# Self-attention on one core: a group's last gathers and the rotation of its keys, each one head later

## The chip, the cores and the metric

The kernel runs on one core of a Trainium2 chip. The time is device time in microseconds of one execution, and the median of several executions is compared. The core's engines work side by side, each through its own instructions in order: TensorE (PE, with weight loads PEld), VectorE (DVE), ScalarE (ACT), GpSimd (POOL) and SyncE (SP, which here only issues DMAs). They wait for each other through semaphores.

## The reference

One decoder layer in float32 on 32 sequences of 64 tokens with 512 features, taken as 2048 tokens: self-attention, cross-attention and a feed-forward part, each with a residual and a layer norm behind it. The change lies in self-attention:

```
NH, NKV, HD = 32, 8, 128;  BLOCK, NBLK, TOPK = 32, 128, 16
q, k, v = x @ wq.T, x @ wk.T, x @ wv.T          # 32, 8 and 8 heads of 128
q, k = apply_rope(q), apply_rope(k)             # one rotation for all tokens
k_full = concat(k_cache[block_idx], k[0])       # 16 cached blocks of 32 keys,
v_full = concat(v_cache[block_idx], v[0])       # and the 64 tokens of sequence 0
attn = softmax(q @ k_full.T / sqrt(HD))         # 576 keys for each query
out = (attn @ v_full) @ wo.T
```

Four query heads share one key and value head. The cached keys and values are the same for all tokens, so they are fetched once for each of the 8 groups.

## The kernel before, in words

Self-attention takes 128 steps, the loop `for n in range(N)`. A step is one head of one block of 512 tokens: 8 groups `g`, in each 4 blocks of tokens `tb`, in each 4 heads `h`. In the text a step's place within its group is `r = n % 16`, called head 0 to head 15.

A head has four tiles of 128 queries. `scores(n, i)` multiplies one tile with the 576 keys into a PSUM tile `s` of two banks (L615), of which the pool `sc` has two; DVE takes the negated maximum (`nmax`, L620); ACT takes the exponential into `p` (L623) and sums it; DVE inverts the sum (`den`, L632), scales `p` by it (L633), and transposes `p` in 32x32 blocks into `T` (L641). `move` issues DMAs that lay `T` out as `pT`, and two heads later `values` multiplies `pT` with the values into `po` (L661). Between the four tiles stand steps of two projections, at L282: the queries of the next block (`q_...`, one step `q`) and the output projection of the last block (`w_...`, step `w`). Both are Strassen-like products of seven multiplications, whose sums of operands are made on POOL: `token_sums` gives `tx` (L196 to L199) at the end of each block, `output_sums` gives `so` (L256 to L259), and the sums of a new group's output weights `wo` come at heads 5 and 6. DVE reads the products back into `qT` and `acc` (L299 to L325, L345, L353).

While group `g` is computed, the keys and values of group `g + 1` are made ready:

- `load_group` at head 4 loads the two weight slices on ACT's queue.
- `gather_keys(g + 1, t)` makes row indices on DVE (`row`, L538, one column for each `t`) and issues an indirect DMA on POOL that fetches 128 rows of cached keys into `kn` (L523). `gather_values(g + 1, t)` does the same for the values into `v`. There are four of each, `t` = 0 to 3. The keys' call stands at the start of a head, the values' between its tiles 2 and 3.
- `rotate(g + 1)` turns the 4 x 128 gathered keys: POOL multiplies the odd elements (L557), DVE makes three products (L558 `kq`, L559 `kr`, L560 `kt`), POOL subtracts (L561), DVE adds (L562).
- `new_keys` (twelve small matmuls, L576 and L582, and two copies on ACT) and `cached_keys` (transposes of the rotated keys, L596) are put into the list `later`, from which `spare_bank` takes one in every even head, after the first step.

PE and DVE run in the order in which the code is written (`manual_schedule` with these two engines). The order of POOL, ACT and SP is made by the scheduler of the framework from dependencies and place in the code. On POOL in head 7 of a group with gathers it is: token sums L197 and L198, gather of keys, gather of values, token sum L199, rotation product L557; then in head 8 the output sum L258 and the rotation's L561.

Of the kernel before, what the change touches and what calls it, by code (L numbers as in the profile page):

```python
# [18 lines left out]
NH, NKV, HD = 32, 8, 128  # L19
REP = NH // NKV  # L20
# [32 lines left out]
def decoder_layer(  # L53
# [49 lines left out]
    def token_room(b, name):  # L103
        return act.tile([P, NC, TB], F32, tag=f"xT{b % 2}", name=name)

    def load_features(dst, src, tb, queue=nc.sync):
        queue.dma_start(
            out=dst, in_=src[:, tb * TB : (tb + 1) * TB].rearrange("(c p) n -> p c n", p=P)
        )
# [9 lines left out]
    def bank(shape, name, tag=None):  # L119
        if tag in special:  # L120
            v = special[tag]
            return v.rearrange("p (a b) -> p a b", a=shape[1])
        return psum[-1].tile(shape, F32, tag=tag or "ps", name=name)
# [340 lines left out]
    with ExitStack() as ph:  # L464
# [47 lines left out]
        def load_group(g, queue=nc.scalar):  # L512
            ws = []
            for tag, src in (("wk", wkT), ("wv", wvT)):
                w = kv.tile([P, NC, HD], F32, tag=tag, name=f"{tag}{g}", bufs=1)
                queue.dma_start(
                    out=w, in_=src[:, g * HD : (g + 1) * HD].rearrange("(c p) n -> p c n", p=P)
                )
                ws.append(w)
            wkv_cur[g] = ws  # L520

        def gather(g, dst, src, t):
            nc.gpsimd.indirect_dma_start(  # L523
                out=dst[:, t, :], out_offset=None, in_=src,
                in_offset=bass.IndirectOffsetOnAxis(ap=rows_cur[g][:, t : t + 1], axis=0),
            )

        def gather_keys(g, t):
            if t == 0:
                rows_cur[g] = kv.tile([P, NKT], I32, tag="row", name=f"row{g}")  # L530
                kn_cur[g] = kv.tile([P, NKT, HD], F32, tag="kn", name=f"kn{g}", bufs=1)
                kr_cur[g] = kv.tile([P, NKT, HD], F32, tag="kr", name=f"kr{g}", bufs=1)
                vs[g] = kv.tile([P, NKC, HD], F32, tag="v", name=f"v{g}")
            if g == 0:
                if t == 0:
                    nc.vector.tensor_scalar(rows_cur[g], row_f, 0.0, None, ALU.add)
            else:
                nc.vector.tensor_scalar(  # L538
                    rows_cur[g][:, t : t + 1], row_f[:, t : t + 1], float(g), None, ALU.add
                )  # L540
            gather(g, kn_cur[g], k_rows, t)

        def gather_values(g, t):
            gather(g, vs[g], v_rows, t)

        def rotate(g, t0=0, t1=NKT):


            kn = kn_cur[g][:, t0:t1, :].rearrange("p t (d two) -> p t d two", two=2)
            k4 = kr_cur[g][:, t0:t1, :].rearrange("p t (d two) -> p t d two", two=2)  # L550
            shape = [P, t1 - t0, HD // 2]
            c3 = cs[:, None, :].to_broadcast(shape)
            s3 = sn[:, None, :].to_broadcast(shape)
            tmp = kv.tile(shape, F32, tag="tmp", name=f"kt{g}_{t0}", bufs=1)
            tmq = kv.tile(shape, F32, tag="tmq", name=f"kq{g}_{t0}", bufs=1)
            e, o = kn[:, :, :, 0], kn[:, :, :, 1]
            nc.gpsimd.tensor_tensor(k4[:, :, :, 1], o, c3, ALU.mult)  # L557
            nc.vector.tensor_tensor(tmq, e, s3, ALU.mult)  # L558
            nc.vector.tensor_tensor(k4[:, :, :, 0], e, c3, ALU.mult)  # L559
            nc.vector.tensor_tensor(tmp, o, s3, ALU.mult)  # L560
            nc.gpsimd.tensor_tensor(k4[:, :, :, 1], k4[:, :, :, 1], tmq, ALU.subtract)  # L561
            nc.vector.tensor_tensor(k4[:, :, :, 0], k4[:, :, :, 0], tmp, ALU.add)  # L562
# [29 lines left out]
        def cached_keys(g, tag="po1"):  # L592
            kr = kr_cur.pop(g)
            pt = bank([P, NKT, P], f"pkt{g}", tag)
            for t in range(NKT):
                nc.tensor.transpose(pt[:, t, :], kr[:, t, :], ident)  # L596
            dst = kTs[g].rearrange("p (s b k) -> p s b k", s=2, k=SQ)
            for r0, b0 in ((0, 0), (2, SHARED + 1)):
                nc.scalar.activation(
                    dst[:, :, b0 : b0 + NKT, :],  # L600
                    pt[:, :, r0 * SQ : (r0 + 2) * SQ].rearrange("p t (s k) -> p s t k", s=2),
                    AF.Copy, scale=SCALE,
                )
# [96 lines left out]
        def columns(g):  # L700
            return slice(g * REP * HD, (g + 1) * REP * HD)
# [39 lines left out]
        def flush():  # L741
            while reads:
                reads.pop(0)()
# [55 lines left out]
        def last_products(i):  # L799
            if i == 3:  # L800
                first.mul("z", 3)
                reads.append(lambda: nc.vector.tensor_tensor(c[0, 1], z, c[0, 1], ALU.add))
            elif i == 7:
                first.mul("y", 7)
                reads.append(lambda: nc.vector.tensor_tensor(c[1, 1], y, c[1, 1], ALU.add))
            else:
                first.mul("y", 4)
                reads.append(lambda: nc.vector.tensor_tensor(c[1, 0], y, c[1, 0], ALU.add))
# [6 lines left out]

        for n in range(N):
            b, h = divmod(n, REP)
            g, r = units[n][0], n % PER  # L820
            if r == REP and g + 1 < NKV:
                load_group(g + 1)
            if r // REP == 1 and g + 1 < NKV:
                gather_keys(g + 1, h)
            if r == 2 * REP and g + 1 < NKV:
                rotate(g + 1)
                later.append(lambda g=g: new_keys(g + 1))
            if r == 2 * REP + 1 and g + 1 < NKV:
                later.append(lambda g=g: cached_keys(g + 1))
            if n == N - REP:  # L830
                encT[0] = big.tile([P, NC, TB], F32, tag="qT", name="encT0", bufs=2)
                load_features(encT[0], encT_in, 0)
            steps = {0: "qwqw", 1: "qw q", 2: "wqwq", 3: "w qw"}[h]

            def step(place):
                if n < REP:

                    i = {(0, 0): 3, (0, 1): 7, (0, 3): 4}.get((n, place))
                    if i:
                        last_products(i)  # L840
                    elif (n, place) in ((0, 2), (1, 0), (1, 1), (1, 2), (1, 3), (2, 0), (2, 2)):
                        q_step(n)
                elif steps[place] == "q":
                    q_step(n)
                elif steps[place] == "w":
                    w_step(b - 2 if h < 2 else b - 1)
                flush()

            def spare_bank():

                if n % 2 == 0 and later:
                    later.pop(0)()

            scores(n, 0)
            step(0)
            spare_bank()
            scores(n, 1)
            if 0 < n < REP:

                move(n - 1, (3,), nc.scalar)  # L860
            if n >= 2:
                values(n - 2, 0, 2 if n % 2 == 0 else 3)
            step(1)
            scores(n, 2)
            step(2)
            if r // REP == 1 and g + 1 < NKV:
                gather_values(g + 1, h)
            scores(n, 3)
            if n >= 2:
                values(n - 2, 2 if n % 2 == 0 else 3, NKT)  # L870
                if n % 2:
                    shared_values(n - 2)
            step(3)
            spare_bank()
            if h == REP - 1:
                if b + 2 < NB:
                    g2, tb2, _ = units[(b + 2) * REP]
                    if tb2 == 0:
                        wq_cur[g2] = load_left(wqT[:, columns(g2)], f"wq{g2}", nc.gpsimd)
                    tok[b + 2] = token_sums(xTs.pop(b + 2), f"tx{g2}_{tb2}", nc.gpsimd)  # L880
                elif b + 2 == NB:
                    kvw[0] = load_kv_left(0, "wq")
                else:
                    encR[0] = token_sums(encT[0], "te0", nc.gpsimd)
            if h == REP - 1 and b + 3 < NB or n == 0:

                b2 = b + 3 if n else 2
                xTs[b2] = token_room(b2, f"xT{b2}")
                load_features(xTs[b2], xT_in, b2 % NTB)
            move(n, (0, 1, 2) if n < REP - 1 else range(NQD))  # L890
# [47 lines left out]
    with ExitStack() as ph:  # L938
# [283 lines left out]
        for n in range(N + 1):  # L1222
            if n < N:
                g, tb = units[n]
# [106 lines left out]
```

## Time and profile before

| | us |
|---|---|
| median of 3 runs | 3100.44 (3098.5 to 3103.58) |
| the profiled execution | 3099.28 |
| its span, first to last instruction | 3097.0 |
| PE busy | 3038.2 (98%) |
| DVE busy | 2184.0 (71%) |
| POOL busy | 967.6 (31%) |
| the scaling of p at L633, 512 times, median and longest of one | 0.520, 2.970 |
| a gather of keys on POOL, 32 times, median; from issue to landing | 0.958; 5.9 to 7.2 |

The page gives for each engine the time in which it was busy, and for groups of instructions the mean of one and the idle time of the engine before them. A line of the timeline has the start, the duration, the engine, the line of the kernel, the operation, what it writes and reads, shapes and count, and in brackets the idle time before it with the instruction that ended it. A line of the view of waits has who waited for whom, the total in us, how often, and the longest. Spans on POOL are rough.

### The profile page before, as it was taken

To read this page: it belongs to the slowest core of one execution; us is meant where nothing else is said; L and a number is where in the kernel's file an instruction comes from. 1 tells how busy PE (TensorE), PEld (TensorE's weight loads), DVE (VectorE), ACT (ScalarE), POOL (GpSimd) and SP (SyncE) were. 2 spreads that over 40 slices of the span, in tenths; PEclk is the share of its full clock that TensorE was granted. 3 is DMA by queue.
4 is the path that set the end of the run, shared out by engine and by line. 5 is a ranking of instruction groups with operands and counts; after the bars stand their busy time and mean duration, and the time that the engine had idled before them with its cause. 6 is when DMAs were issued, how large, how long until landed. Compare 5 with 4: busy or idle time off the path is not lost.

```text
span 3097.0 us, 42303 instructions
## 1 busy us (share of the span) xinstructions
PE 3038.2 (98%) x14944; PEld 2318.1 (75%) x14944; DVE 2184.0 (71%) x3957; ACT 754.8 (24%) x1760; POOL 967.6 (31%) x789
## 2 busy tenths in 40 slices
PE   8999999999999999999999999999999999999998
PEld 6777677777777777777677769988888888888864
DVE  6777777877877877877877754346656656656777
ACT  2323222222222232232322321211111111111132
POOL 4231321321322322323222122135444444444421
PEclk9999999999999999999999999999999999999999
DMA  6444444444444444444344343321121121121101
GB/s 206 116 114 119 113 115 123 111 122 114 108 128 112 106 128 113 107 125 118 101 123 109 98 126 128 109 103 48 50 67 48 51 66 48 51 66 48 49 28 41
DMA packets 200913, 298.66 MB, mean 96 GB/s; under 512 B 44160, under 2 KB 94848, under 8 KB 200704
## 3 DMA queue, kind: packets, MB, share of 16 engines
q1 hardware_dynamic: 187328, 282.51, 33.7%
q10 hardware_dynamic: 11328, 9.26, 1.0%
q0 software_dynamic: 2048, 4.20, 0.5%
q8 instruction: 120, 1.97, 0.3%
q14 instruction: 89, 0.73, 0.1%
HBM read 107.05 MB, written 20.97 MB: 41 GB/s over the span
## 4 chain that ended last, share of the span: by engine, by line
PE 86%; DVE 10%; DMA 1%; SPq 1%; issue 1%; ACT 1%; DVEq 0%; ACTq 0%
PE po L661 15%; PE s L615 15%; PE pox L1103 2%; DVE acc L345 2%; SPq L653 1%; PE w_0y L282 1%; PE q_3y L282 1%; PE w_3y L282 1%; PE qx_3y L282 1%; PE qx_2y L282 1%; PE qx_0y L282 1%; PE q_2y L282 1%; PE w_1y L282 1%; PE qx_1y L282 1%; PE wx_3y L282 1%; PE q_0y L282 1%
## 5 line engine op out<-in xcount | busy, mean ns | idle before, releaser
L623 ACT ACTIVATE p<-s,nmax 128x576 f32<-128x576 f32 x512 | 379.2, 741 | 1211.6 <-DVE nmax L620 1173.1
L615 PE MATMUL s<-kT,qT 128*128 128x288 f32 x2048 | 578.0, 408 | 11.5 <-ACT p L623 10.7
L661 PE MATMUL po<-pT,v 128*128 128x512 f32 (+1 forms) x1280 | 549.1, 602 | 4.3 <-DMA pT<-T 4.3
L615 PEld LDWEIGHTS s<-kT,qT 128*128 128x128 f32 x2048 | 387.4, 190 | 116.4 <-issue 20.1
L620 DVE TENSOR_REDUCE nmax<-s 128x1 f32<-128x576 f32 x512 | 384.0, 750 | 47.5 <-PE s L615 45.3
L641 DVE STREAM_TRANSPOSE T<-p 128x576 f32<-128x576 f32 x512 | 394.0, 769 | 4.4
L661 PEld LDWEIGHTS po<-pT,v 128*128 128x128 f32 (+1 forms) x1280 | 213.7, 189 | 204.2 <-issue 176.9
L633 DVE TENSOR_SCALAR p<-p,den 128x576 f32<-128x576 f32 x512 | 325.5, 636 | 17.9
L632 DVE RECIPROCAL den<-den 128x1 f32<-128x1 f32 x512 | 83.9, 164 | 238.2 <-ACT p L623 220.0
L256 POOL TENSOR_TENSOR so<-oT,oT 128x512 f32<-128x512 f32 x32 | 42.6, 1330 | 651.0 <-ACT oT L684 651.0
L258 POOL TENSOR_TENSOR so<-oT 128x512 f32<-128x512 f32 x32 | 40.7, 1272 | 334.4 <-PE w_1y L282 93.0
L1209 POOL TENSOR_TENSOR txx<-x1T 128x512 f32<-128x512 f32 x31 | 39.3, 1267 | 244.4 <-PE qx_3z L282 94.1
L197 POOL TENSOR_TENSOR tx<-xT 128x512 f32<-128x512 f32 x31 | 39.7, 1280 | 206.9 <-PE q_3z L282 65.5
L623 ACT ACTIVATION_READ_ACCUMULATOR p<-s,nmax 128x1 f32 x512 | 99.0, 193 | 0.0
L1059 ACT ACTIVATE ex<-ex 128x512 f32<-128x512 f32 x64 | 39.3, 630 | 203.1 <-DVE ex L1058 203.1
L256 POOL TENSOR_TENSOR sox<-oTx,oTx 128x512 f32<-128x512 f32 x32 | 40.5, 1266 | 149.7 <-DVE oTx L1123 144.3
L684 ACT COPY oT<-po 128x512 f32<-128x512 f32 x128 | 71.8, 586 | 44.9 <-PE po L661 44.1
L1043 PEld LDWEIGHTS sx<-kvx,qTx 128*64 128x64 f32 x2048 | 62.3, 138 | 10.6 <-issue 10.6
L1121 ACT ACTIVATE oTx<-pox,bv 128x256 f32<-128x256 f32 x128 | 52.0, 470 | 66.4 <-PE pox L1103 66.4
L1043 PE MATMUL sx<-kvx,qTx 128*64 128x64 f32 x2048 | 66.7, 224 | 0.0
L1103 PE MATMUL pox<-pTx,kvx 64*128 64x256 f32 x512 | 64.5, 389 | 0.1
L1123 DVE TENSOR_SCALAR oTx<-pox,bv 128x256 f32<-128x256 f32 x128 | 53.6, 478 | 9.8 <-PE pox L1103 9.8
(445 smaller groups left out, 5779.9 us busy)
## 6 DMA issues: line engine op xcount, KB each, us to landing
pT<-T SPq DMA_DIRECT2D x1020, 80.0 KB
pT<-T SPq DMA_DIRECT2D x1016, 64.0 KB
xT<-in_xT SPq DMA_DIRECT2D x31, 1024.0 KB
kvx<-kv SPq DMA_DIRECT2D x32, 512.0 KB
pTx<-Tx SPq DMA_DIRECT2D x256, 64.0 KB
kv<-c SPq DMA_DIRECT2D x30, 512.0 KB
wo<-in_woT SPq DMA_DIRECT2D x32, 256.0 KB
xwq<-in_xwq SPq DMA_DIRECT2D x32, 256.0 KB
```

The source lines that it names most:

```text
L256: nc.gpsimd.tensor_tensor(t[1], a[1, 0], a[1, 1], ALU.add)
L282: nc.tensor.matmul(self.banks[b][:, m, :], self.left[i][:, k, m * P : (m + 1) * P], self.right[i][:, k, :], start=(first and m + k == 0), ...
L615: nc.tensor.matmul(s[:, a, :HALF], qTs[n // REP][:, units[n][2], i * P : (i + 1) * P], kTs[g][:, a * HALF : (a + 1) * HALF], start=True, s ...
L620: nc.vector.tensor_reduce(nmax, s[:, :, :HALF], AX.XY, ALU.max, negate=True)
L623: nc.scalar.activation(p.rearrange("q (a k) -> q a k", a=2), s[:, :, :HALF], AF.Exp, bias=nmax, accum_out=den,)
L632: nc.vector.reciprocal(den, den)
L633: nc.vector.tensor_scalar(p, p, den, None, ALU.mult)
L641: nc.vector.transpose(Ts[n][:, :, i, :], ps_.pop((n, i)).rearrange("q (b k) -> q b k", k=SQ))
L661: nc.tensor.matmul(pos[n].rearrange("d (a q) -> d a q", a=NQD), vs[units[n][0]][rows, v, :], pTs[n // 2][rows, :, chunk, :], skip_group_ch ...
L684: nc.scalar.copy(o[:, i, :].rearrange("d (t a k) -> d a t k", t=TPB, a=NQD), pos.pop(n - 1 + i).rearrange("d (a t k) -> d a t k", a=NQD, t ...
L1043: nc.tensor.matmul(s[b * SEQ : (b + 1) * SEQ, i * REP + h, :], qTs[n][:, h, pr * HF + c0 : pr * HF + c0 + SEQ], kvs[n][:, pr, 0, c0 : c0 + ...
L1103: nc.tensor.matmul(po[pr, b][:, i, :].rearrange("d (h a j) -> d h a j", h=REP, a=2), kvs[n][r, pr, 1, i * HD : (i + 1) * HD], pTs[n][r, :, ...
```

## The change

Four steps of the preparation are placed otherwise, in each of the seven groups that prepare a next one. The gathers of keys and values number 3 go from head 7, the last of the second block of tokens, to head 8, the first of the third block. The rotation goes from the start of head 8 to the start of head 9. Gathers 0 to 2 stay at heads 4 to 6, the new keys at head 8, the transposes of the cached keys at head 10.

```
+        gathers = {4: 0, 5: 1, 6: 2, 8: 3}
         for n in range(N):
             b, h = divmod(n, REP)
             g, r = units[n][0], n % PER
             if r == REP and g + 1 < NKV:
                 load_group(g + 1)
-            if r // REP == 1 and g + 1 < NKV:
-                gather_keys(g + 1, h)
+            if r in gathers and g + 1 < NKV:
+                gather_keys(g + 1, gathers[r])
             if r == 2 * REP and g + 1 < NKV:
-                rotate(g + 1)
                 later.append(lambda g=g: new_keys(g + 1))
             if r == 2 * REP + 1 and g + 1 < NKV:
+                rotate(g + 1)
                 later.append(lambda g=g: cached_keys(g + 1))
...
-            if r // REP == 1 and g + 1 < NKV:
-                gather_values(g + 1, h)
+            if r in gathers and g + 1 < NKV:
+                gather_values(g + 1, gathers[r])
```

As built, no instruction is added or dropped, and the orders of PE and of SP's queue are the same. On DVE the last row index (L538) goes from the start of head 7 to that of head 8, and the rotation's four operations from the start of head 8 to that of head 9. On POOL head 7 has the three token sums alone; the output sum L258 of head 8 is followed by the gather of keys, the gather of values, and the rotation's L557 and L561. On ACT the copy of the first query product (L310) goes behind the exponential of head 8's first tile.

## The prediction

> A measurement of this kernel can tell about 0.2% (6.2 us) from no change; the chances below use that bound. Heads are numbered 0 to 15 inside a group (four blocks of four heads), groups 0 to 7, and s(7,1) is tile 1 of head 7. +x is a time from the start of a head, which is its first score matmul.
>
> **What bounds the kernel now.** First the shares and the chain of waits:
>
> ```profile
> PE 3038.2 (98%) x14944; PEld 2318.1 (75%) x14944; DVE 2184.0 (71%) x3957; ACT 754.8 (24%) x1760; POOL 967.6 (31%) x789
> ...
> PE 86%; DVE 10%; DMA 1%; SPq 1%; issue 1%; ACT 1%; DVEq 0%; ACTq 0%
> ```
>
> TensorE (PE) is busy for 98% of the span, so moving work on other engines gains only where PE stands still; that is 59 us in all (3097.0 - 3038.2). So next, whom PE waits for:
>
> ```profile
> PE s L615 <- ACT p L623: 10.7, 10, 1.2
> ```
>
> Ten waits of a score matmul for an exponential. In the timeline of PE, four are at the start and the end of attention; the other six are 1.2 us each, all in one place: head 7 of groups 1 to 6. From score row to score row, head 7 of group 1 lasts from 335.77 to 350.99, 15.22 us; head 7 of group 7, where nothing is gathered for a next group, lasts from 1702.13 to 1715.88, 13.75 us. Groups 2 to 6 have the same 15.22. So PE loses 15.22 - 13.75 = **1.47 us, six times**. The timeline of group 1 shows why:
>
> ```profile
> 338.47 1.13 PE L615 MATMUL s<-kT,qT 128*128 128x288 f32 x4
> ...
> 338.91 0.13 DVE L538 TENSOR_SCALAR row<-row_f 128x1 int32<-128x1 f32 x1
> ...
> 340.58 0.94 POOL L523 DMA_INDIRECT v<-in_v_cache,row  x1 [0.30 <-issue]
> ...
> 340.87 2.97 DVE L633 TENSOR_SCALAR p<-p,den 128x576 f32<-128x576 f32 x1
> ...
> 341.54 1.27 POOL L199 TENSOR_TENSOR tx<-xT,tx 128x512 f32<-128x512 f32 x1
> ...
> 342.77 0.74 POOL L557 TENSOR_TENSOR kr<-kn,cs 128x256 f32<-128x256 f32 x1
> ...
> 344.35 0.74 DVE L620 TENSOR_REDUCE nmax<-s 128x1 f32<-128x576 f32 x1
> ...
> 345.19 0.74 ACT L623 ACTIVATE p<-s,nmax 128x576 f32<-128x576 f32 x1 [4.55 <-DVE nmax L620]
> ...
> 346.07 0.78 PEld L615 LDWEIGHTS s<-kT,qT 128*128 128x128 f32 x4 [1.60 <-ACT p L623]
> 346.07 1.24 PE L615 MATMUL s<-kT,qT 128*128 128x288 f32 x4 [1.20 <-ACT p L623]
> ```
>
> Read it backwards. s(7,3) needs one of two score banks, which the exponential of (7,1) frees; that waits for its maximum; and the maximum stands on DVE behind the scaling of (7,0), which took 2.97 us where the median of 512 is 0.52. Beside the long one, GpSimd (POOL) ran three instructions without a gap: the gather of values, a token sum, the first product of the rotation.
>
> [...] 2.97 instead of 0.52 us beside POOL arithmetic, and the first rotation product of group 0 (two SBUF inputs) took 1.05 instead of 0.53 beside a POOL sum. It also shows that a gather alone does not do it: in head 4 of group 1 the scaling at 296.67 took 0.52 us beside the gather of values at 296.59. [...] bars of 0.94 to 0.96 us, landings 5.9 to 7.2 us after issue.
>
> **The change, part by part.** No instruction is added or removed. Per group, seven times, it moves one row-index operation (DVE 0.13 us), two gathers (POOL 0.96 + 0.94 us, 128 rows each) and the rotation (DVE four operations, POOL two, 0.74 + 0.79 us). The orders of PE and of SP's queue are the same in the two built programs.
>
> *Head 7.* POOL had: two token sums, gather of keys, gather of values, third token sum, first rotation product. It keeps the three token sums; the gathers and the product go behind the next block's first output sum. The third token sum then follows the second, which ends at 338.73, and is over at about 340.0, before the scaling at 340.87. So the scaling should take 0.52 us and everything after it on DVE comes 2.97 - 0.52 = 2.45 us sooner: the exponential of (7,1), over at 346.02, is over at 343.6. s(7,3) can start at +8.94, which is 344.71 (the place of s(7,3) in group 0, 118.45 - 109.51). The spare is 1.1 us. Even if the scaling met the third token sum, it would be as in group 7:
>
> ```profile
> 1705.08 1.27 POOL L199 TENSOR_TENSOR tx<-xT,tx 128x512 f32<-128x512 f32 x1
> ...
> 1705.49 1.17 DVE L633 TENSOR_SCALAR p<-p,den 128x576 f32<-128x576 f32 x1
> ```
>
> 1.17 us, and head 7 lasted 13.75 there. Gain: 6 x 1.47 = **8.8 us**. Group 0 has no such wait (13.75 already) and gains nothing.
>
> *Head 8.* It lasts 16.28 us in all seven groups without a gap on PE: 14.22 plus 2.06 for the new keys' matmuls. Taking the rotation out of it gains nothing. Into it come the row index and two gathers. The same row index and gathers stand at the same place of head 4 in the kernel before (row at +0.81, gather at +1.73, after the same output sum and just behind a load of tokens), with no wait on PE. Cost 0. The first rotation product now starts when the keys land, about +9, and may delay one scaling by up to 0.74 us; PE's extra 2.06 us covers that. On ACT one copy of queries goes behind an exponential that is no longer late: 0. On POOL the output sum now stands ahead of the gathers and waits for nothing new.
>
> *Head 9.* This is the only place that the trace before does not show: the rotation on DVE in a head without new keys. Its price is read in head 8:
>
> ```profile
> 353.37 0.53 DVE L558 TENSOR_TENSOR kq<-kn,sn 128x256 f32<-128x256 f32 x1
> ...
> 355.15 0.42 DVE L562 TENSOR_TENSOR kr<-kr,kt 128x256 f32<-128x256 f32 x1
> 355.50 0.75 DVE L620 TENSOR_REDUCE nmax<-s 128x1 f32<-128x576 f32 x1
> ```
>
> 355.50 - 353.37 = 2.13 us ahead of the maximum of (9,0), and behind it all of head 9's softmax. It will begin 0.57 after the accumulation (352.80 to 353.37), that is at +0.77, so the maximum moves from +1.17 to +2.90: 1.73 later. Head 9 before:
>
> ```profile
> 367.27 1.13 PE L615 MATMUL s<-kT,qT 128*128 128x288 f32 x4
> ...
> 372.23 0.74 ACT L623 ACTIVATE p<-s,nmax 128x576 f32<-128x576 f32 x1 [2.11 <-DVE nmax L620]
> ...
> 375.44 0.69 DVE L345 TENSOR_TENSOR acc<-w_0z,acc 128x512 f32<-128x512 f32 x1 [1.62 <-PE w_0z L282]
> ```
>
> The exponential of (9,1) is read out at 373.06, +5.79; it moves to +7.52, and s(9,3), which needs its bank, starts at +8.94. The spare is 1.4 us. The 1.62 us for which DVE was idle before 375.44 then swallow the delay, so nothing passes to head 10. The rotated keys are next wanted for head 10's transposes, over 13 us later. The keys land by about +9.2 of head 8 (2.0 + 7.2), and the rotation begins 16.28 + 0.77 = 17.05 after its start: 8 us to spare. I take 0 for head 9. Bounds: not below 0, as PE has no gap there; above, the whole 2.13 us if nothing covers it, 7 x 2.13 = 14.9 us.
>
> **Sum.** The profiled execution took 3099.28 us (span 3097.0 and 2.3 around it). 3099.28 - 8.8 = 3090.5. The median of the runs, 3100.44, lies 1.16 above that execution, so the forecast is 3100.44 - 8.8 = **3091.6 us**.
>
> **Rivals.**
> 1. *The stall shrinks but stays* (0.17, with runs that scatter). DVE enters head 7 about 1.7 us behind its place in group 0 (maximum at +3.19 against +1.45), because scalings in head 6 (1.56) and at its end (1.17) met POOL sums that are not moved. If the scaling of (7,0) meets more than the third token sum, half the stall may be left: 3100.4 - 4.4 = 3096. For it: that lateness. Against it: after the third token sum POOL has nothing until the output sum some 10 us later.
> 2. *The rotation loses its cover* (0.09), the one that ends slower. In head 8 the 2.06 us of new-key matmuls hid it; head 9 has none. It decides once the exponential of (9,1) ends after +8.94, which takes 1.4 us on DVE beyond the 2.13: a scaling of (9,0) as long as the one seen in head 7 would do. If the whole 2.13 us fell on PE: 7 x 2.13 - 8.8 = +6.1, 3106.5 us. Against it: POOL's second rotation product (0.79) is over before that scaling, and POOL then waits for the end of head 9.
> 3. *The change doesn't do what it says* (0.02): POOL's order is a scheduler's; but in the built program the gathers do stand behind the output sum. It would give 3100.
>
> **How the numbers follow.** The full gain has 0.72: 3091.6, with some 2.5 us on either side (the three runs before reach 1.9 below and 3.1 above their median). Most of that is beyond 0.2% (below 3094.2). Adding what part of rival 1 passes the bound: faster 0.75, within 0.2% 0.16, slower 0.09. The range starts at 3088.5 and reaches to 3097, into rival 1; rival 2 is left out.
>
> **What would show it.** Right: the wait of s for p on PE falls from 10.7 to about 3.5 us, all of it outside groups 1 to 6; head 7 of these groups 13.75 us, heads 8, 9, 10 unchanged at 16.28, 13.75, 14.66; the longest scaling at L633 far below 2.97. Step by step: gathers at about +2 of head 8, rotation on DVE at +0.77 of head 9, exponential of (9,1) before +8.94. Wrong: a new wait of s(9,3) for p in head 9 of seven groups, or a scaling of 2 us or more in head 8 or 9 beside POOL arithmetic.

## The result, and the profile after

The changed kernel takes 3090.51 us (median of 8 runs, 3089.06 to 3093.27), the kernel before 3100.16 (8 runs, 3098.5 to 3103.58). The ratio is 0.997, with a 95% interval from 0.996 to 0.998: some 9 us faster. The forecast was 3091.6. The profiled execution took 3090.08 us, its span is 3088.3, which is 8.7 shorter than before. One execution of a later kernel, that with all row indices at once, took 11576.58 us at a granted clock of 0.518; the ratios leave it out, and why it was slow is not known.

First the same two lines of the page as before, the shares and the chain:

```profile
PE 3034.1 (98%) x14944; PEld 2316.4 (75%) x14944; DVE 2171.2 (70%) x3957; ACT 755.3 (24%) x1760; POOL 967.5 (31%) x789
...
PE 86%; DVE 10%; DMA 1%; SPq 1%; issue 1%; ACT 1%; DVEq 0%; POOL 0%; ACTq 0%; POOLq 0%
```

They hardly differ, and would not tell that anything happened: a gain of 0.3% is not seen in shares. DVE is busy for 12.8 us less although it runs the same 3957 instructions; 11.0 us of it are scalings at L633 (325.5 before, 314.4 after) and 1.3 us the rotation's first product, both for time in which they were held up, which the profile counts as busy: the scaling of (7,0) has a bar of 2.97 us before and of 0.52 now. The view of whom PE waits for does tell:

```profile
PE s L615 <- ACT p L623: 3.1, 4, 1.1
```

The ten waits of 10.7 us are four of 3.1 us, all at the start and end of attention. In groups 1 to 6 PE waits for nothing in head 7, which lasts 13.75 us in all of them, against 15.22 before: 6 x 1.47 = 8.8 us. That the two spans differ by 8.7 is luck in part: this execution was already 1.74 us ahead when head 7 of group 0 began (107.77 against 109.51), and it lost 1.9 us elsewhere, in heads 12 and 13 of some groups and behind attention. Heads 8, 9 and 10 last 16.28, 13.75 and 14.66, as before. The timeline of head 7 in group 1 (it begins at 334.41):

```profile
336.00 1.37 POOL L198 TENSOR_TENSOR tx<-xT,tx 128x512 f32<-128x512 f32 x1
...
337.45 1.27 POOL L199 TENSOR_TENSOR tx<-xT,tx 128x512 f32<-128x512 f32 x1
...
339.45 0.52 DVE L633 TENSOR_SCALAR p<-p,den 128x576 f32<-128x576 f32 x1
...
340.48 0.75 DVE L620 TENSOR_REDUCE nmax<-s 128x1 f32<-128x576 f32 x1
...
341.33 0.74 ACT L623 ACTIVATE p<-s,nmax 128x576 f32<-128x576 f32 x1 [2.11 <-DVE nmax L620]
...
343.35 1.13 PE L615 MATMUL s<-kT,qT 128*128 128x288 f32 x4
```

The third token sum (L199) follows the second and is over at 338.72; the scaling of (7,0) begins 0.7 us after that, takes 0.52 us instead of 2.97, and s(7,3) starts at +8.94 with no idle time in its brackets. What left head 7 is found in heads 8 and 9 (head 8 begins at 348.16), first on POOL, then on DVE:

```profile
349.92 0.96 POOL L523 DMA_INDIRECT kn<-in_k_cache,row  x1 [0.16 <-issue]
351.18 0.95 POOL L523 DMA_INDIRECT v<-in_v_cache,row  x1 [0.30 <-issue]
355.58 0.74 POOL L557 TENSOR_TENSOR kr<-kn,cs 128x256 f32<-128x256 f32 x1 [3.46 <-DMA kn<-in_k_cache,row]
365.81 0.79 POOL L561 TENSOR_TENSOR kr<-kr,kq 128x256 f32<-128x256 f32 x1 [9.49 <-DVE kq L558]
```

```profile
351.47 0.52 DVE L633 TENSOR_SCALAR p<-p,den 128x576 f32<-128x576 f32 x1
...
365.25 0.41 DVE L558 TENSOR_TENSOR kq<-kn,sn 128x256 f32<-128x256 f32 x1
...
367.25 0.75 DVE L620 TENSOR_REDUCE nmax<-s 128x1 f32<-128x576 f32 x1
...
372.61 0.69 DVE L345 TENSOR_TENSOR acc<-w_0z,acc 128x512 f32<-128x512 f32 x1
```

The scaling of (8,0) at 351.47 runs beside the gather of values in 0.52 us. The longest of the 512 scalings is now 1.60 us. The rotation takes 367.25 - 365.25 = 2.00 us of head 9, which begins at 364.44, and the 1.62 us that DVE stood idle before the accumulation there are gone: the delay went into them, and PE saw nothing of it.

### The profile page after: what moved, and what is told of

It is laid out like the page before. It is cut to its first block, busy times and chain, and to the rows that moved or that the text cites. A ratio compares the mean times of both kernels' runs of the same rounds, so it can differ in the third digit from the quotient of the medians.

```text
span 3088.3 us, 42296 instructions
## 1 busy us (share of the span) xinstructions
PE 3034.1 (98%) x14944; PEld 2316.4 (75%) x14944; DVE 2171.2 (70%) x3957; ACT 755.3 (24%) x1760; POOL 967.5 (31%) x789
## 4 chain that ended last, share of the span: by engine, by line
PE 86%; DVE 10%; DMA 1%; SPq 1%; issue 1%; ACT 1%; DVEq 0%; POOL 0%; ACTq 0%; POOLq 0%
PE po L661 16%; PE s L615 15%; PE pox L1106 2%; DVE acc L345 2%; PE q_3y L282 1%; PE w_0y L282 1%; PE w_3y L282 1%; PE qx_3y L282 1%; PE qx_2y L282 1%; PE qx_0y L282 1%; PE w_1y L282 1%; PE q_2y L282 1%; DVE ex L1066 1%; PE q_0y L282 1%; PE w_2y L282 1%; PE wx_3y L282 1%
## 5 line engine op out<-in xcount | busy, mean ns | idle before, releaser
L633 DVE TENSOR_SCALAR p<-p,den 128x576 f32<-128x576 f32 x512 | 314.4, 614 | 17.9
L258 POOL TENSOR_TENSOR so<-oT 128x512 f32<-128x512 f32 x32 | 40.7, 1272 | 343.0 <-PE w_1y L282 93.0
```

What stands on the lines that cost most here:

```text
L633: nc.vector.tensor_scalar(p, p, den, None, ALU.mult)
```

## The experiments

The theory, P: the scaling of (7,0) was held up by POOL's run of gather, token sum and rotation product, and the change gains by taking the first and last away from it. The rivals: R1, the gain comes from the rotation leaving head 8; R2, the maximum of (7,1) is late because DVE enters head 7 late; R4, the rotation need not have moved. Times of heads are from first score matmul to first score matmul, in groups 1 to 6.

### The rotation alone

```
             if r == 2 * REP and g + 1 < NKV:
-                rotate(g + 1)
                 later.append(lambda g=g: new_keys(g + 1))
             if r == 2 * REP + 1 and g + 1 < NKV:
+                rotate(g + 1)
                 later.append(lambda g=g: cached_keys(g + 1))
```

> The kernel before with the rotation alone moved to head 9; gathers number 3 stay in head 7. As built, GpSimd in head 7 keeps the gathers, the third token sum and the first rotation product, in the old order. Theory P (the scaling of (7,0) is held up by GpSimd's work in head 7): head 7 of groups 1 to 6 stays at 15.2 us, the scaling at L633 stays near 2.97 us, time 3100 us, no change. Rival R1 (the gain came from taking the rotation's 2.1 us of VectorE out of head 8): 3091 us. If the rotation lost its cover in head 9: up to 3115 us.

3098.24 us, ratio 0.9999 (0.999 to 1.0007): no change. Head 7 stays at 15.22 us in five groups and is 14.60 in the last. The view of waits of PE, then POOL and DVE in head 7 of group 1:

```profile
PE s L615 <- ACT p L623: 9.6, 10, 1.2
```

```profile
340.02 0.94 POOL L523 DMA_INDIRECT v<-in_v_cache,row  x1 [0.31 <-issue]
340.99 1.27 POOL L199 TENSOR_TENSOR tx<-xT,tx 128x512 f32<-128x512 f32 x1
342.22 0.74 POOL L557 TENSOR_TENSOR kr<-kn,cs 128x256 f32<-128x256 f32 x1
```

```profile
340.31 2.97 DVE L633 TENSOR_SCALAR p<-p,den 128x576 f32<-128x576 f32 x1
```

The product stays in head 7 although the code now asks for it two heads later: the scheduler puts it where its keys are there. R1 falls. Head 9 is 13.75 us here too, with the rotation in it. In group 6, the last of the six, the scaling took 2.35 us and ended while the product ran, and the product took 1.03 us instead of 0.74; why, the runs do not show.

### The gathers alone

```
             if r == 2 * REP and g + 1 < NKV:
+                rotate(g + 1)
                 later.append(lambda g=g: new_keys(g + 1))
             if r == 2 * REP + 1 and g + 1 < NKV:
-                rotate(g + 1)
```

(against the changed kernel)

> The changed kernel with the rotation put back to the start of head 8, right behind the call that gathers keys number 3. Head 7 is as in the changed kernel, so theory P gives 13.75 us there. But VectorE's first rotation product now waits for the keys, which land 6.2 to 7.3 us after head 8 begins in the changed kernel; the maximum of (8,0) then starts at about +9.4 instead of +1.4, its exponential ends at about +11, and s(8,2), due at +9.17, is 1 to 2.1 us late in seven groups: head 8 17.3 to 18.4 us, time 3091 + 7 to 15 = 3098 to 3106 us. Rival R4 (only the gathers' move matters, the rotation could have stayed): 3091 us.

3104.86 us, ratio to the kernel before 1.0018 (1.0008 to 1.0028): slower than either. Head 7 is 13.75 us, as P says; head 8 is 17.6 to 18.1 us in four groups and 20.6 in two, and stays at 16.28 in group 0, where the last keys landed 2.5 us after their gather had begun, against 4.2 to 5.6 in the others. DVE and PE in group 1:

```profile
355.07 0.43 DVE L558 TENSOR_TENSOR kq<-kn,sn 128x256 f32<-128x256 f32 x1 [6.03 <-DMA kn<-in_k_cache,row]
```

```profile
359.36 2.29 PE L615 MATMUL s<-kT,qT 128*128 128x288 f32 x4 [2.46 <-ACT p L623]
361.44 2.50 PE L282 MATMUL q_3x<-xT,wq 128*128 128x256 f32 x8
```

DVE stands for 6.03 us at the head of its queue for keys that have just been asked for, and everything of the softmax stands behind it. So R4 falls: the rotation's move gains nothing by itself, and without it the gathers' move loses more than it gains. The two worst groups, whose keys landed last, lost more than forecast; see the last section.

### The one scaling on ScalarE

```
-            nc.vector.tensor_scalar(p, p, den, None, ALU.mult)
+            if i == 0 and n % PER == 7 and g + 1 < NKV:
+                nc.scalar.activation(p, p, AF.Copy, scale=den)
+            else:
+                nc.vector.tensor_scalar(p, p, den, None, ALU.mult)
```

(against the kernel before)

> The kernel before with one scaling in each of the seven groups, that of (7,0), done by ScalarE instead of VectorE; nothing else moves, GpSimd's work in head 7 stays. Theory P: the maximum of (7,1) no longer stands behind a blocked scaling, head 7 goes to 13.75 us, 3091 us as in the changed kernel, the maximum of (7,1) about 2.4 us sooner. Rival R2 (the maximum is late because VectorE enters head 7 late, or for the row index ahead of it): head 7 stays near 15.2 us, 3100 us.

3088.02 us, ratio 0.997 (0.9958 to 0.9983). ACT in head 7 of group 1:

```profile
339.91 0.78 ACT L634 ACTIVATE p<-p,den 128x576 f32<-128x576 f32 x1 [0.23 <-DVE den L632]
341.16 0.74 ACT L623 ACTIVATE p<-s,nmax 128x576 f32<-128x576 f32 x1 [0.47 <-DVE nmax L620]
```

Head 7 begins at 334.81 here. With POOL's work left in place and DVE entering head 7 just as late (maximum of (7,0) at +3.19), the maximum of (7,1) starts at +5.56 instead of +8.58 and head 7 is 13.75 us. R2 falls: the lateness alone does no harm; the one blocked scaling is the whole of it. (This kernel also takes 0.52 us off DVE. The changed kernel does not, its maximum of (7,0) is as late, at +3.14, and that of (7,1) starts at +6.07, which is early enough.)

### The product on VectorE

```
-            nc.gpsimd.tensor_tensor(k4[:, :, :, 1], o, c3, ALU.mult)
+            (nc.vector if g else nc.gpsimd).tensor_tensor(k4[:, :, :, 1], o, c3, ALU.mult)
```

(against the kernel before)

> The kernel before with the first rotation product (L557) on VectorE in groups 1 on, at its place in head 8; GpSimd in head 7 keeps both gathers and the third token sum. It splits GpSimd's three pieces. If the gather of values and the token sum together hold the scaling until the sum ends (about +7.0): scaling about 2.2 us, s(7,3) still 0.6 late, head 7 about 14.4 us, 3096 us. If a gather alone does not hold it: scaling 0.52 us, it ends before the token sum begins, head 7 13.75 us, 3091 us. If only the gather matters: the scaling is short of 1.2 us. Head 8 has 0.42 us more on VectorE, which is covered: 16.28 us.

3094.99 us, ratio 0.9987 (0.998 to 0.9994). Head 7 is 14.53 us, head 8 16.28. From the timeline of group 1:

```profile
340.03 0.95 POOL L523 DMA_INDIRECT v<-in_v_cache,row  x1 [0.30 <-issue]
...
340.32 2.28 DVE L633 TENSOR_SCALAR p<-p,den 128x576 f32<-128x576 f32 x1
341.00 1.27 POOL L199 TENSOR_TENSOR tx<-xT,tx 128x512 f32<-128x512 f32 x1
```

The scaling ends at 342.60, 0.33 us after the bar of the sum (its stretch in the profile). In the kernel before it ended 0.33 us after that of the product (343.84 and 343.51). So it was held until about the end of the last of POOL's pieces. Of the 2.45 us lost, the product is worth 2.97 - 2.28 = 0.69, the other two 2.28 - 0.52 = 1.76.

### The gathers with nothing behind them

The product on VectorE as above, and the third token sum of head 7 on VectorE at the end of that head:

```
-        eng.tensor_tensor(t[4], b21, t[2], ALU.subtract)
+        (last or eng).tensor_tensor(t[4], b21, t[2], ALU.subtract)
...
+                        xTs.pop(b + 2), f"tx{g2}_{tb2}", nc.gpsimd, last=nc.vector if r == 7 else None
```

> The kernel before with the third token sum of head 7 and the first rotation product done by VectorE (at the end of head 7 and in head 8). GpSimd in head 7 keeps two token sums and both gathers, and nothing behind the gathers. It measures a gather alone against a scaling: the scaling of (7,0) starts 0.3 us into the gather of values. If the gather alone holds it until its end: 1.1 to 1.3 us. If not: 0.52 us. Either way s(7,3) is not late: head 7 13.75 us, head 8 16.28 us with VectorE's 1.1 us more covered, time 3091 us.

3091.59 us, ratio 0.9976 (0.9966 to 0.9987); heads 7 and 8 at 13.75 and 16.28. POOL's last gather, then DVE, in head 7 of group 1:

```profile
339.03 0.95 POOL L523 DMA_INDIRECT v<-in_v_cache,row  x1 [0.30 <-issue]
```

```profile
339.33 0.52 DVE L633 TENSOR_SCALAR p<-p,den 128x576 f32<-128x576 f32 x1
```

The same gather, the same 0.3 us into it, and the scaling takes 0.52 us in all groups. This kernel differs from the one above only in the sum. So the gather alone costs DVE nothing here. With the sum right behind the gather, in the kernel above, the scaling that began at 340.32 was not over after 0.52 us, at 340.84, although the sum's bar begins only at 341.00.

### All row indices at once

`gather_keys` makes all four columns at `t == 0` in one operation (against the kernel before).

> The kernel before with all four columns of row indices of a group made at once at head 4, so that a gather waits for no index on VectorE. As built, GpSimd then issues all eight gathers and the first rotation product back to back in heads 4 and 5, and head 7 has the three token sums alone. Theory P, with gathers that alone do not hold a scaling: head 7 13.75 us, time as the changed kernel, 3091 us. If eight gathers in a row hold the scalings of head 4 (some 10 us): heads 4 or 5 1 us or more longer, 3097 us or more.

3090.92 us, ratio 0.997 (0.9959 to 0.9982). Head 7 is 13.75 us, heads 4 and 5 are as before (14.22 and 13.75). POOL in heads 4 and 7 of group 1:

```profile
302.02 0.94 POOL L523 DMA_INDIRECT kn<-in_k_cache,row  x1 [0.30 <-issue]
303.27 0.94 POOL L523 DMA_INDIRECT v<-in_v_cache,row  x1 [0.30 <-issue]
304.85 0.74 POOL L552 TENSOR_TENSOR kr<-kn,cs 128x256 f32<-128x256 f32 x1 [0.63 <-DMA kn<-in_k_cache,row]
...
337.66 1.27 POOL L199 TENSOR_TENSOR tx<-xT,tx 128x512 f32<-128x512 f32 x1
```

Here gathers and product leave head 7 in the other direction, the rotation stays in head 8, and the gain is the same: it is head 7 without them that counts, not heads 8 and 9 with them. The eight gathers in a row, 10 us, left the scalings of heads 4 and 5 at 0.52 to 0.70 us. DVE is also on time in head 7 here (maximum of (7,0) at +1.47), so this kernel says nothing about R2.

### How much head 9 can hold

The third rotation product is written two or seven times more, same values, in the changed kernel:

```
-            nc.vector.tensor_tensor(tmp, o, s3, ALU.mult)
+            for _ in range(3 if g else 1):      # 8 in the second
+                nc.vector.tensor_tensor(tmp, o, s3, ALU.mult)
```

> The changed kernel with the third product of the rotation written two times more in each group, same values: 0.7 to 0.9 us more on VectorE at the start of head 9. In the changed kernel the exponential of (9,1) is read out at +7.43 and s(9,3) starts at +8.94, a spare of 1.5 us. If that spare is real, 0.9 us fits: head 9 stays at 13.75 us, time as the changed kernel, 3090.5 us. Rival 2 (VectorE's time in head 9 has no cover): 7 x 0.8 = 5 to 6 us more, 3096 us.

3090.45 us, ratio 0.9973 (0.9962 to 0.9985), as the changed kernel. The maximum of (9,0) starts 0.93 us later (+3.74 instead of +2.81), the exponential of (9,1) is read out at +8.36, and head 9 lasts 13.75 us.

> The same with the product written seven times more: 2.4 to 3.0 us more on VectorE in head 9, which is 0.9 to 1.5 us over the spare of 1.5 us. The exponential of (9,1) at about +10 then ends after s(9,3) is due at +8.94: head 9 14.8 to 15.4 us in seven groups, a wait of s for p in each, time 3090.5 + 7 to 11 = 3098 to 3102 us, and the rotation at head 9 would have been no gain. If the spare is larger than it reads: 3090.5 us.

3105.82 us, ratio 1.0022 (1.0014 to 1.003). DVE in head 9 of group 1, and PE's waits:

```profile
367.96 4.18 DVE L561 TENSOR_TENSOR kt<-kn,sn 128x256 f32<-128x256 f32 x8
```

```profile
PE s L616 <- ACT p L624: 14.5, 11, 1.6
```

The products cost more than I had put, 3.22 us on DVE instead of 2.4 to 3.0, and head 9 and the time came out above what was expected. The exponential of (9,1) ends at +10.65, s(9,3) starts at +10.70, and head 9 is 15.62 us in seven groups: 7 x 1.87 = 13.1 us, of the 13.7 by which the span grew (3102.0 - 3088.3). So 0.93 us goes free and 3.22 us costs 1.76 at s(9,3): the spare is what it reads, 1.5 us.

### The two best side by side

> The changed kernel once more, beside the next one on the same chip. If both have the same heads (13.75 us for head 7 and no wait of PE anywhere in groups 1 to 6), their medians agree within 1.5 us, about 8 to 9 us below the kernel before.

> The kernel before with the scaling of (7,0) on ScalarE, once more, to tell whether its 3088 us on another chip was better than the changed kernel's 3090.5. By the heads there is nothing left to gain: within 1.5 us of the changed kernel. If it is really faster: 2 us or more below it.

On one chip: changed kernel 3090.41 us (ratio 0.9975, 0.9965 to 0.9985), scaling on ScalarE 3089.43 (0.997, 0.9958 to 0.9982). They are not told apart. No version is shown to beat the changed kernel, and by its trace little is left for one of this kind: in the 1372 us from 320 to 1692, groups 1 to 6, PE is busy for 1371.66.

## Why the prediction was right, point by point

*Where PE loses.* 6 x 1.47 us in head 7, forecast as the whole gain. Measured 8.8 us in those heads, and 8.7 in the span. Right.

*The cause.* A scaling of 2.97 us beside POOL's work. The scaling on ScalarE shows that this one instruction is the cause, and the kernels that take the product, and then also the sum, away from POOL show which POOL work: 0.69 us for the product, 1.76 for gather and token sum together, 0 for a gather alone. The prediction had a gather alone at nothing from one line in head 4; that held. Why the scaling was held from the moment it was issued, 0.7 us before the sum's bar, no run shows.

*Head 7 after.* Third token sum over at about 340.0, which is +4.2: measured +4.3. Exponential of (7,1) 2.45 us sooner: +7.75 instead of +10.25, 2.50. In group 0 the scaling did meet the third token sum (1.23 us) and the head kept its 13.75, as the case of group 7 had said.

*Head 8.* Cost 0 for two gathers and a row index at its start: right, the scaling beside them took 0.52. The landing was mis-sized. The "landings 5.9 to 7.2 us after issue", in the table of the kernel before too, rest on two of the 32 gathers, the only ones whose landing that trace holds, at 5.0 and 7.5 us of the whole program; they gave +9.2. In the trace before, the product ran 3.45 us after its last gather had begun (342.77 - 339.32), so those keys had landed sooner. In the changed kernel, where the trace has all 32, the median is 2.9 us, and gather number 3 in head 8 took 4.2 to 6.1 us in groups 1 to 6; in group 1 the product ran 5.66 us after it (355.58 - 349.92), at +7.4. The error was on the safe side and touched no sum. The product then met the scaling of (8,1) in two groups, for 0.11 us, where up to 0.74 had been allowed.

*Head 9.* The one place that could only be worked out: maximum of (9,0) at +2.90 (measured +2.81), exponential of (9,1) at +7.52 (+7.43), spare 1.4 us (1.5), cost 0 (13.75 us in all groups). The rotation took 2.00 instead of 2.13 us; the difference lies in its first product, which has no POOL sum beside it now (0.41 instead of 0.53). The two padded kernels show that the spare is real and where it ends.

*The rivals.* Half a stall left: no, DVE's late entry into head 7 (+3.14) stayed and did no harm. The rotation loses its cover: its deciding point was right, 1.4 us beyond the rotation, as the second padded kernel crossed it and was slower than the kernel before. The price that the rival was given, all of 2.13 us, was too simple: of 3.22 us more, with a spare of 1.5, PE lost 1.76.

## What to carry to other kernels

Where a short DVE operation has a long maximum in its row, look at what GpSimd does in that stretch before looking at DVE itself; here arithmetic without gaps, right behind a gather, held a scaling of 0.52 us until 0.33 us after the end of the last piece (2.97 us with the product, 2.28 without it), and beside a gather alone it took its 0.52. A piece of preparation is moved together with what follows from it: with the last gathers and the operation that uses them in one head VectorE stood still for 6.03 us with all its queue, and with the operation one head later it did not. And idle time of an engine ahead of a wait can take work free: in head 9 the rotation's 2.00 us cost PE nothing, nor did 0.93 us more, and 3.22 us more cost 1.76 where the spare was 1.5. Read the spare from the first instruction of the bottleneck that needs the result, not from shares.

## What the runs showed that I had not expected

A gap of PE can have a second price. In the kernel with the gathers alone PE stood for 2.46 us in group 1 and 2.33 in group 4, and for 1.07 to 1.51 in the other four. In the stretches around the first gap, the granted clock (the number behind POOL's busy time) is:

```profile
346.00:358.00 12.00, 10.89 (x60) 8.31 (x59) 5.59 (x11) 2.85 (x7) 4.96 (x5) 1.00 0.76 198
358.00:366.00 8.00, 6.64 (x19) 4.80 (x20) 6.39 (x14) 2.97 (x7) 0.00 (x0) 0.79 0.40 97
366.00:372.00 6.00, 6.00 (x27) 4.89 (x26) 4.39 (x10) 1.66 (x4) 0.00 (x0) 1.00 0.23 54
```

The clock averaged 0.79 over the 8 us from 358 to 366, in which the gap ends (359.36), and 1.00 before and after them. The four score matmuls at 359.36 took 2.29 us instead of 1.13. Head 8 of groups 1 and 4 lost 4.3 us each (20.6 - 16.28), where the others lost 1.3 to 1.8. My estimate for group 1: 8 x (1 - 0.79) = 1.7 us for the slower clock, which with the gap of 2.46 makes 4.2.

The length of a gap alone does not decide it. In the changed kernel PE stood for 2.08 us at the end of attention (1811.44 to 1813.53), and the clock was 1.00 from 1813.60 to 1817.00. Near the end of the program it stood for 1.83 us (3053.74 to 3055.57), and the clock was 0.51 from 3055.60 to 3059.00. What decides, no run here shows.
